# A transformer block's FFN in another order: the first row's gates ahead of the second row's products, the last row finished tile by tile, and the last sums on GpSimd

## The chip, the cores and the metric

The kernel runs on one core of one Trainium2 chip. Its engines work side by side, each through its own list of instructions: TensorE (PE, with its weight loads shown apart as PEld), VectorE (DVE), ScalarE (ACT) and GpSimd (POOL); SyncE (SP) issues most of the DMAs. The metric is the device time of one execution in microseconds (us); lower is better.

## What is computed

One transformer block on x of shape (2, 512, 512), all in float32: attention with 32 heads of 128, and then a feed-forward part that is a base product plus a gated mixture of eight low-rank experts. Each half is taken of the layer norm of x, and its own layer norm is added to x. Cut to what the change touches:

```python
def ffn(x, W_base, b_base, W_gate, W_thr, b_thr, A, B):
    base = x @ W_base.T + b_base
    adapted = softmax(x @ W_gate.T) - sigmoid(x @ W_thr.T + b_thr) / 8
    weights = maximum(adapted, 0)
    wsum = weights.sum(-1, keepdims=True)
    weights = weights / where(wsum == 0, 1, wsum)
    h = einsum('nd,erd->ner', x, A)          # 8 experts of rank 16
    return base + 2 * einsum('ner,ne,eor->no', h, weights, B)

x = x + layernorm(attention(layernorm(x)))
x = x + layernorm(ffn(layernorm(x)))
```

## The kernel before, in words

The two rows of the batch, b = 0 and 1, are each cut into NT = 4 tiles of 128 tokens by 512 features; NK = 4 is the number of 128-blocks of the feature dimension. The projections, the sums of the weights and the 64 rounds of attention (a round is one head of one row) come first and fill the first 1236 us. The change touches only what follows in `attention()` after the last round.

The block is built under a schedule in which PE, DVE, ACT and GpSimd run their instructions in the order in which the program writes them. So an instruction that waits holds back everything written after it on its engine, and "earlier in the text" means "earlier on the engine". Only SP's DMAs are placed by the scheduler.

PSUM, where PE leaves its products, is used as eight buffers of 128x512: four with the tag "ps" and four with the tag "aux" (`pt`). Each tag is a ring: the fifth tile of a tag takes the buffer of the first one, and its product waits until that one has been read.

The steps after the last round, for each row b:

- `outward` (L658): the last group's four products with Wo for each tile, psy; the sum `y` (L666) adds them to what earlier groups left.
- `residual` (called with "r"): `norms` over the four tiles of y, and then y = y * rs + (x + shift). This is the x of the second half, and stays in y.
- `norm_transposed`: `norms` again, ACT writes the normalized tile n_f, PE transposes its four blocks (nt_f), and four copies bring these out as nT_f, two by DVE (L164) and two by ACT (L166).
- the gate products hg (L798): one tile of 128 x 137 for each token tile: 128 hidden values h, 8 gate logits, 1 threshold. ACT copies them to hs (L801).
- the base products f (L806): four products for each token tile, left open in PSUM.
- the gates: a reduction for the maximum, two exponentials on ACT, some fourteen short DVE instructions, and then hw = h times its expert's weight for each token tile (L844).
- hT: PE transposes the four hw, ACT copies them out as hwT (L853).
- the expert products (L856): one more product on each of the four open f.
- z (L858): DVE adds the bias row; then `residual` with "z", whose result goes out by one DMA for each token tile (L862).

`norms` is a generator that all of these share. For each tile it issues bn_stats and bn_aggr on DVE and a square root on ACT (L144), and one tile later a reciprocal (L133) and the product `shift` = -mean * rs (L135) on DVE. `shift` is a scalar_tensor_tensor of 128x1: its two tensor inputs are the mean and rs.

Row 0's `ffn` uses "ps" for its transposes and its f, row 1's uses "aux" for its transposes; hg and hT use "aux" for both, and f uses "ps" for both. The second row's psy are in "aux", and their sums y are written behind the first row's copies nT_f. `ffn` is a generator in four parts, and the loop at the end of `attention()` interleaves the two rows with

```python
for part in (second, first, first, second, second):
    next(part)
```

that is: transposes of row 1, gates and hT of row 0, expert products of row 0, gate and base products of row 1, gates and hT of row 1, and then the rest of row 0 and of row 1. In it row 0's z statistics come on DVE behind row 1's gates, and row 1's four z come before any of its statistics.

ACT loads a table when its function changes between square root and exponential (ACT_TABLE_LOAD); copies and Identity need none. GpSimd has nothing to do after the last maximum of the attention (L528).

Of the kernel before, what the change touches and what calls it, by code (L numbers as in the profile page):

```python
# [9 lines left out]
F32 = mybir.dt.float32  # L10
AF = mybir.ActivationFunctionType
ALU = mybir.AluOpType
AX = mybir.AxisListType

P = 128
# [15 lines left out]
def kernel(ctx: ExitStack, tc: tile.TileContext, x, wq, wk, wv, wo, vecs, rows, wbase, gates, bexp, out):  # L31
# [33 lines left out]
    def tt(name):  # L65
        return tmp.tile([P, 512], F32, tag="tmp", name=name)

    def wide(name):
        return spool.tile([P, NT, 512], F32, tag="wide", name=name)
# [3 lines left out]
    def pt(name, tag=None):  # L73
        if tag is None:
            tag = ("ps", "aux")[turn_of[0] % 2]
            turn_of[0] += 1
        return psum.tile([P, 512], F32, tag=tag, name=name)
# [49 lines left out]
    def norms(srcs, name):  # L127

        waiting = []

        def ready():
            i, mv, rs = waiting.pop(0)
            nc.vector.reciprocal(rs, rs)  # L133
            shift = small.tile([P, 1], F32, tag="shift", name=f"shift_{name}_{i}")
            nc.vector.scalar_tensor_tensor(shift, mv[:, 0:1], -1.0, rs, ALU.mult, ALU.mult)  # L135
            return i, rs, shift

        for i, src in enumerate(srcs):
            st = small.tile([P, 6], F32, tag="st", name=f"st_{name}_{i}")
            mv = small.tile([P, 2], F32, tag="mv", name=f"mv_{name}_{i}")  # L140
            nc.vector.bn_stats(st, src)
            nc.vector.bn_aggr(mv, st)
            rs = small.tile([P, 1], F32, tag="rs", name=f"rs_{name}_{i}")
            nc.scalar.activation(rs, mv[:, 1:2], AF.Sqrt, bias=epst[:, 0:1], scale=1.0)  # L144
            waiting.append((i, mv, rs))
            if i > 0:
                yield ready()
        yield ready()

    def norm_transposed(tiles, name, tag):  # L150

        n = wide(f"n_{name}")
        pss = [pt(f"nt_{name}_{c}", tag) for c in range(NK)]
        for i, rs, shift in norms(tiles, name):
            nc.scalar.activation(n[:, i, :], tiles[i], AF.Identity, bias=shift, scale=rs)
            for c in range(NK):
                nc.tensor.transpose(pss[c][:, ts(i, P)], n[:, i, ts(c, P)], ident)

        def tiles_of():
            outs = []  # L160
            for c in range(NK):
                o = npool.tile([P, 512], F32, tag="nT", name=f"nT_{name}_{c}")
                if c % 2 == 0:
                    nc.vector.tensor_copy(o, pss[c])  # L164
                else:
                    nc.scalar.copy(o, pss[c])  # L166
                outs.append(o)
            return outs

        return tiles_of  # L170
# [134 lines left out]
    def attention():  # L305
# [351 lines left out]
        def y_tile(b, t):  # L657
            return y_pairs[b, t // 2][:, t % 2, :]  # L658

        def outward(g, b, t, tag=None):  # L660

            ps = pt(f"psy{b}_{g}_{t}", tag or "aux")
            for j in range(GH):
                o = os[b, g * GH + j]
                nc.tensor.matmul(ps, o[:, ts(t, P)], wos[g][j], start=(j == 0), stop=(j == GH - 1))  # L665
            return lambda: nc.vector.tensor_tensor(y_tile(b, t), ps, y_tile(b, t), ALU.add)  # L666
# [80 lines left out]
        )  # L747
        nc.sync.dma_start(out=gate_sb, in_=gates.rearrange("(c p) f -> p c f", p=P))
        nc.sync.dma_start(out=bexp_sb, in_=bexp)
        adds = [outward(NG - 1, 0, t, "ps") for t in range(NT)]  # L750
        for add in adds:
            add()
        adds = [outward(NG - 1, 1, t, "aux") for t in range(NT)]
        for b in range(B):
            x2 = [y_tile(b, t) for t in range(NT)]
            for _ in residual(again[b], x2, f"r{b}"):
                pass
            if b == 0:
                first = ffn(0, x2, wb, gate_sb, bexp_sb)
                next(first)  # L760
                for add in adds:
                    add()
                next(first)
            else:
                second = ffn(1, x2, wb, gate_sb, bexp_sb)

                for part in (second, first, first, second, second):
                    next(part)
                for _ in first:
                    pass  # L770
                for _ in second:
                    pass

    def residual(xts, ys, name):

        waiting = []

        def add():
            i, rs = waiting.pop(0)
            nc.vector.scalar_tensor_tensor(ys[i], ys[i], rs, xts[i], ALU.mult, ALU.add)  # L780
            return i

        for i, rs, shift in norms(ys, name):
            nc.scalar.activation(xts[i], xts[i], AF.Identity, bias=shift, scale=1.0)
            if waiting:
                yield add()
            waiting.append((i, rs))
        yield add()

    def ffn(b, xs, w, gate_sb, bexp_sb):  # L790

        xT = norm_transposed(xs, f"f{b}", "ps" if b == 0 else "aux")()
        yield
        hs = wide(f"hs{b}")[:, :, 0 : E * R + E + 1]
        for t in range(NT):
            ps = pt(f"hg{b}_{t}", "aux")
            for c in range(NK):
                nc.tensor.matmul(  # L798
                    ps[:, 0 : E * R + E + 1], xT[c][:, ts(t, P)], gate_sb[:, c, :], start=(c == 0), stop=(c == NK - 1)
                )  # L800
            nc.scalar.copy(hs[:, t, :], ps[:, 0 : E * R + E + 1])  # L801
        pss = []
        for t in range(NT):
            ps = pt(f"f{b}_{t}", "ps")
            for c in range(NK):
                nc.tensor.matmul(ps, xT[c][:, ts(t, P)], w[:, c, :], start=(c == 0), stop=False)  # L806
            pss.append(ps)
        yield

        def sm(name, n=NT):  # L810
            return small.tile([P, n], F32, tag=name, name=f"{name}{b}", bufs=1)

        def per_token(v):
            return v.unsqueeze(2).to_broadcast([P, NT, E])

        gl = hs[:, :, E * R : E * R + E]
        mx = sm("gmx")
        nc.vector.tensor_reduce(mx, gl, AX.X, ALU.max)
        ew = small.tile([P, NT, E], F32, tag="ew", name=f"ew{b}", bufs=1)
        nc.vector.tensor_tensor(ew, gl, per_token(mx), ALU.subtract)  # L820
        nc.scalar.activation(ew, ew, AF.Exp)
        thr = sm("thr")
        nc.scalar.activation(thr, hs[:, :, E * R + E], AF.Exp, bias=nbthr, scale=-1.0)
        nc.vector.tensor_scalar(thr, thr, 8.0, 8.0, ALU.mult, ALU.add)
        nc.vector.reciprocal(thr, thr)
        se = sm("gse")
        nc.vector.tensor_reduce(se, ew, AX.X, ALU.add)
        nc.vector.reciprocal(se, se)
        nc.vector.tensor_tensor(ew, ew, per_token(se), ALU.mult)
        nc.vector.tensor_tensor(ew, ew, per_token(thr), ALU.subtract)  # L830
        nc.vector.tensor_scalar(ew, ew, 0.0, None, ALU.max)
        ws = sm("gws")
        nc.vector.tensor_reduce(ws, ew, AX.X, ALU.add)
        iz = sm("giz")
        nc.vector.tensor_scalar(iz, ws, 0.0, None, ALU.is_equal)
        nc.vector.tensor_tensor(ws, ws, iz, ALU.add)
        nc.vector.reciprocal(ws, ws)
        nc.vector.tensor_scalar(ws, ws, 2.0, None, ALU.mult)
        nc.vector.tensor_tensor(ew, ew, per_token(ws), ALU.mult)

        pst = pt(f"hT{b}", "aux")
        for t in range(NT):
            hw = tt(f"hw{b}_{t}")
            nc.vector.tensor_tensor(  # L844
                hw[:, 0 : E * R].rearrange("p (e r) -> p e r", r=R),
                hs[:, t, 0 : E * R].rearrange("p (e r) -> p e r", r=R),
                ew[:, t, :].unsqueeze(2).to_broadcast([P, E, R]),
                ALU.mult,
            )
            nc.tensor.transpose(pst[:, ts(t, P)], hw[:, 0:P], ident)  # L850
        yield
        hT = tt(f"hwT{b}")
        nc.scalar.copy(hT, pst)  # L853
        zs = []
        for t in range(NT):
            nc.tensor.matmul(pss[t], hT[:, ts(t, P)], bexp_sb, start=False, stop=True)  # L856
            z = opool.tile([P, 512], F32, tag="o", name=f"z{b}_{t}")
            nc.vector.tensor_tensor(z, pss[t], bbase_b, ALU.add)  # L858
            zs.append(z)
        yield  # L860
        for t in residual(xs, zs, f"z{b}"):
            nc.sync.dma_start(out=out[b, ts(t, P), :], in_=zs[t])  # L862

    with tc.manual_schedule(engines=IN_ORDER):
        attention()
# [36 lines left out]
```

## Time and profile before

| | |
|---|---|
| three runs | 1334.28, 1334.54, 1338.74 us (median 1334.54) |
| the profiled execution | 1335.98 us |
| its span, first to last instruction | 1334.0 us |
| mean granted PE clock | 0.993 |
| busy: PE, DVE, ACT, POOL | 97%, 73%, 40%, 35% of the span |
| last round's weighted sum to the first transposes of row 0 | 1233 to 1264 us |
| from there to the end of the last product | 1264 to 1323 us |
| from there to the end of the span | 1323 to 1334 us |

The profile names an instruction by its line, engine and operation, and by the tiles that it writes and reads ("hT<-ident,hw" is the transposition of hw into hT). An f32 product appears as two records, so 16 products are "x32". A releaser (<-) is the instruction that ended a wait. Records of PE overlap a little and their ends are modelled; so the starts of the next ones are the safer measure.

The instructions of 128x512 elements that this part of the kernel is made of, from the page and the groups by form (mean, us): DVE sums 0.69, bn_stats 0.68, the DVE sum with a factor (scalar_tensor_tensor, L780) 0.75, ACT's normalization n_f 0.81, ACT copies 0.59, ACT's Identity with a shift 0.72, GpSimd's sums of the projections (L236) 1.30 and 1.38. A table load takes 1.28.

### The profile page before, as it was taken

To read this page: it belongs to the slowest core of one execution; us is meant where nothing else is said; L and a number is where in the kernel's file an instruction comes from. 1 tells how busy PE (TensorE), PEld (TensorE's weight loads), DVE (VectorE), ACT (ScalarE), POOL (GpSimd) and SP (SyncE) were. 2 spreads that over 40 slices of the span, in tenths; PEclk is the share of its full clock that TensorE was granted. 3 is DMA by queue.
4 is the path that set the end of the run, shared out by engine and by line. 5 is a ranking of instruction groups with operands and counts; after the bars stand their busy time and mean duration, and the time that the engine had idled before them with its cause. 6 is when DMAs were issued, how large, how long until landed. Compare 5 with 4: busy or idle time off the path is not lost.

```text
span 1334.0 us, 11818 instructions
## 1 busy us (share of the span) xinstructions
PE 1296.3 (97%) x3532; PEld 651.2 (49%) x3532; DVE 973.7 (73%) x1242; ACT 533.6 (40%) x736; POOL 472.1 (35%) x361
## 2 busy tenths in 40 slices
PE   7999999999999999999999999999999999999976
PEld 3444444444444444455555555555555555544443
DVE  7565654887565478888777787786787898899566
ACT  5222222322311234354454545545454655544333
POOL 4689897555762011111122222222222333211000
PEclk9999999999999999999999999999999999999988
DMA  7789978598997765533456565565656555511001
GB/s 286 245 317 309 342 269 274 198 328 298 334 324 258 249 201 182 180 122 101 153 150 172 152 185 153 144 189 163 161 154 186 146 134 134 127 64 38 26 1 63
DMA packets 146127, 250.45 MB, mean 188 GB/s; under 512 B 11792, under 2 KB 39568, under 8 KB 146064
## 3 DMA queue, kind: packets, MB, share of 16 engines
q1 hardware_dynamic: 135408, 230.31, 51.8%
q0 software_dynamic: 10080, 18.35, 8.4%
q10 hardware_dynamic: 576, 1.05, 0.2%
q8 instruction: 28, 0.46, 0.1%
q14 instruction: 35, 0.29, 0.1%
HBM read 147.43 MB, written 83.89 MB: 173 GB/s over the span
## 4 chain that ended last, share of the span: by engine, by line
PE 64%; DVE 6%; ACT 1%; issue 1%; ACTq 0%; DVEq 0%
PE pss L515 15%; PE o L571 15%; PE v L458 15%; PE psw L621 11%; PE psy L665 2%; PE f L806 2%; PE p_k L215 2%; DVE quarters L534 1%; DVE s L559 1%; ACT s L562 1%; PE f L856 1%; PE hg L798 1%; DVE y L655 1%; PE psd L548 1%; DVE m L525 1%
## 5 line engine op out<-in xcount | busy, mean ns | idle before, releaser
L528 POOL PARTITION_ALL_REDUCE top<-m x64 | 119.0, 1860 | 617.6 <-DVE m L526 617.6
L516 ACT ACTIVATE s<-pss,rk 128x512 f32<-128x512 f32 x256 | 175.9, 687 | 320.1 <-PE pss L515 314.6
L571 PE MATMUL o<-s,v 128*128 128x512 f32 x512 | 231.4, 594 | 5.9 <-ACT s L562 2.6
L515 PE MATMUL pss<-qh,kh 128*128 128x512 f32 x512 | 230.2, 592 | 0.0
L515 PEld LDWEIGHTS pss<-qh,kh 128*128 128x128 f32 x512 | 97.3, 190 | 122.4 <-issue 121.5
L571 PEld LDWEIGHTS o<-s,v 128*128 128x128 f32 x512 | 96.2, 190 | 112.0 <-issue 96.9
L534 DVE TRANSPOSE_TENSOR_REDUCE quarters<-s 128x64 f32<-128x2048 f32 x64 | 147.3, 2302 | 0.0
L559 DVE TENSOR_TENSOR s<-s,top 128x2048 f32<-128x2048 f32 x64 | 146.0, 2282 | 0.0
L562 ACT ACTIVATE s<-s 128x2048 f32<-128x2048 f32 x64 | 121.7, 1902 | 13.7 <-DVE s L559 13.6
L458 PE MATMUL v<-w_v,t 128*128 128x512 f32 x256 | 116.8, 600 | 0.0
L550 DVE RECIPROCAL inv<-psd 128x16 f32<-128x16 f32 x64 | 16.4, 256 | 127.5 <-PE psd L548 127.5
L235 ACT ACTIVATE sq_k<-k 128x512 f32<-128x512 f32 x62 | 38.6, 630 | 137.6 <-DVE k L288 65.8
L236 POOL TENSOR_TENSOR accq<-accq,sq_q 128x512 f32<-128x512 f32 x62 | 80.7, 1303 | 35.5 <-ACT sq_q L235 33.7
L236 POOL TENSOR_TENSOR acck<-acck,sq_k 128x512 f32<-128x512 f32 x62 | 85.4, 1381 | 22.1 <-ACT sq_k L235 19.0
L235 ACT ACTIVATE sq_q<-q 128x512 f32<-128x512 f32 x62 | 38.9, 631 | 134.0 <-DVE q L288 69.2
L458 PE MATMUL v<-w_v,nT_a 128*128 128x512 f32 x192 | 88.3, 601 | 0.0
L621 PE MATMUL psw<-wr,oh 128*128 128x256 f32 x384 | 88.3, 380 | 0.0
L215 PE MATMUL p_k<-t,s_k 128*128 128x512 f32 x192 | 85.0, 592 | 0.0
L215 PE MATMUL p_q<-t,s_q 128*128 128x512 f32 x192 | 85.0, 592 | 0.0
L621 PEld LDWEIGHTS psw<-wr,oh 128*128 128x128 f32 x384 | 72.5, 190 | 19.8 <-issue 11.5
L525 DVE TENSOR_TENSOR m<-s 128x1024 f32<-128x1024 f32 x64 | 77.8, 1216 | 4.7 <-ACT s L516 4.7
L458 PEld LDWEIGHTS v<-w_v,t 128*128 128x128 f32 x256 | 46.7, 190 | 49.3 <-issue 49.0
(180 smaller groups left out, 1774.5 us busy)
## 6 DMA issues: line engine op xcount, KB each, us to landing
keptq<-q SPq DMA_DIRECT2D x64, 256.0 KB, 6.5
q<-keptq SPq DMA_DIRECT2D x16, 1024.0 KB, 6.5
w_v<-keptw SPq DMA_DIRECT2D x32, 512.0 KB, 4.0
keptk<-k SPq DMA_DIRECT2D x64, 256.0 KB, 6.4
keptqs<-q SPq DMA_DIRECT2D x64, 256.0 KB, 6.6
qh<-keptqs SPq DMA_DIRECT2D x64, 256.0 KB, 3.0
kh<-keptk SPq DMA_DIRECT2D x64, 256.0 KB, 2.7
keptv<-o_v SPq DMA_DIRECT2D x64, 256.0 KB, 3.7
```

The source lines that it names most:

```text
L215: nc.tensor.matmul(ps, a[:, c, ts(j, P)], x[c], start=(c == 0), stop=(c == 1))
L236: nc.gpsimd.tensor_tensor(accs[b], accs[b], sq, ALU.add)
L458: nc.tensor.matmul(ps, x[c][:, ts(t, P)], w[:, c, :], start=(c == 0), stop=(c == 1))
L515: nc.tensor.matmul(ps, kk[i][:, ts(k, P)], qs[i], start=True, stop=True)
L516: nc.scalar.activation(s[:, k, :], ps, AF.Copy, scale=rks[b][:, k : k + 1])
L525: nc.vector.tensor_tensor(m, s[:, 0:2, :], s[:, 2:4, :], ALU.max)
L528: nc.gpsimd.partition_all_reduce(ms[i], m[:, 0, :], P, ReduceOp.max)
L534: nc.vector.tensor_reduce(quarters.rearrange("p k j -> p (k j)"), ss[i].rearrange("p k (j r) -> p (k j) r", r=32), AX.X, ALU.add, apply_tr ...
L559: nc.vector.tensor_tensor(s, s, top.unsqueeze(1).to_broadcast([P, NT, 512]), ALU.subtract)
L562: nc.scalar.activation(ss[i], ss[i], AF.Exp)
L571: nc.tensor.matmul(po, vs[b, c][:, k, ts(j, P)], ss[i][:, k, :], start=(k == 0), stop=(k == NT - 1))
L621: nc.tensor.matmul(ps[:, t, :], a, right_of[i, g][:, j, :], start=(j == 0), stop=(j == 1))
```

## The change

`ffn` becomes a class with one method for each step, and the caller writes out the order. The order at the end of `attention()`:

```diff
-        adds = [outward(NG - 1, 0, t, "ps") for t in range(NT)]
-        for add in adds:
+        x2s = [[y_tile(b, t) for t in range(NT)] for b in range(B)]
+        first, second = (Ffn(b, x2s[b], wb, gate_sb, bexp_sb) for b in range(B))
+        adds = [[outward(NG - 1, b, t, ("ps", "aux")[b]) for t in range(NT)] for b in range(B)]
+        for add in adds[0]:
             add()
-        adds = [outward(NG - 1, 1, t, "aux") for t in range(NT)]
-        for b in range(B):
...
-                for part in (second, first, first, second, second):
-                    next(part)
-                for _ in first:
-                    pass
-                for _ in second:
-                    pass
+        residual(again[0], x2s[0], "r0")
+        first.norm()
+        first.turn()
+        first.gate_products()
+        for add in adds[1]:
+            add()
+        residual(again[1], x2s[1], "r1")
+        first.base(range(NT))
+        second.norm()
+        first.gates()
+        second.turn()
+        first.hidden()
+        second.gate_products()
+        first.experts(range(NT))
+        first_z = list(first.z())
+        second.gates()
+        second.base(range(2))
+        second.hidden()
+        second.base(range(2, 3))
+        second.experts(range(3))
+        second.base(range(3, NT))
+        second.experts(range(3, NT))
+        first.finish(first_z)
+        second.finish(second.z(), direct=(NT - 1,))
```

Transposes, gate products and hT of both rows now use "ps", and the base products of both rows use "aux". Two token tiles share one PSUM tile of gate products, and so one ACT copy:

```diff
+            for u in range(NT // 2):
+                ps = pt(f"hg{b}_{u}", "ps")[:, 0 : 2 * W].rearrange("p (t f) -> p t f", t=2)
...
+                nc.scalar.copy(self.hs[:, ts(u, 2), :], ps)
```

The gates are the same instructions as before, in `gates()`, with the four hw at their end; `hidden()` is the transposes and the copy hwT, now in a tile of `opool`. The finish is new. `z()` is a generator, so that for row 1 each tile's z comes directly before that tile's bn_stats; for row 0 the four z are made at once, as `first_z`. Of the eight last sums seven go to GpSimd, on a z that ACT has normalized in place; the last tile of row 1 keeps the way it had:

```diff
+            for t, rs, shift in norms(coming(), f"z{self.b}"):
+                z, x2 = got[t], self.xs[t]
+                if t in direct:
+                    nc.scalar.activation(x2, x2, AF.Identity, bias=shift, scale=1.0)
+                    nc.vector.scalar_tensor_tensor(z, z, rs, x2, ALU.mult, ALU.add)
+                else:
+                    nc.scalar.activation(z, z, AF.Identity, bias=shift, scale=rs)
+                    nc.gpsimd.tensor_tensor(z, z, x2, ALU.add)
+                nc.sync.dma_start(out=out[self.b, ts(t, P), :], in_=z)
```

As built, GpSimd's list gets, behind the last maximum of the attention, one more unnamed instruction and the seven sums; the lists of the other engines hold the same work in the new order, four copies hs less on ACT, and the stores keep their order on SP.

More of the change, by code (lines that the diff above doesn't have):

```diff
@@ L749, in attention @@
         nc.sync.dma_start(out=bexp_sb, in_=bexp)
-        adds = [outward(NG - 1, 0, t, "ps") for t in range(NT)]
-        for add in adds:
+        x2s = [[y_tile(b, t) for t in range(NT)] for b in range(B)]
+        first, second = (Ffn(b, x2s[b], wb, gate_sb, bexp_sb) for b in range(B))
+        adds = [[outward(NG - 1, b, t, ("ps", "aux")[b]) for t in range(NT)] for b in range(B)]
+        for add in adds[0]:
             add()
-        adds = [outward(NG - 1, 1, t, "aux") for t in range(NT)]
-        for b in range(B):
-            x2 = [y_tile(b, t) for t in range(NT)]
-            for _ in residual(again[b], x2, f"r{b}"):
-                pass
[L758 to L765, printed above, removed]
-                for part in (second, first, first, second, second):
-                    next(part)
-                for _ in first:
-                    pass
-                for _ in second:
-                    pass
+        residual(again[0], x2s[0], "r0")
[22 more added lines that the diff above has]
+        second.finish(second.z(), direct=(NT - 1,))
     def residual(xts, ys, name):
@@ L780, in add @@
             nc.vector.scalar_tensor_tensor(ys[i], ys[i], rs, xts[i], ALU.mult, ALU.add)
-            return i
         for i, rs, shift in norms(ys, name):
@@ L785, in residual @@
             if waiting:
-                yield add()
+                add()
             waiting.append((i, rs))
[L788 to L799, printed above, removed]
-                )
[L801 to L862, printed above, removed]
@@ new lines, in residual, with __init__, norm, turn @@
+        add()
+    class Ffn:
+        def __init__(self, b, xs, w, gate_sb, bexp_sb):
+            self.b, self.xs, self.w, self.gate_sb, self.bexp_sb = b, xs, w, gate_sb, bexp_sb
+            self.pss = {}
+        def norm(self):
+            self.turned = norm_transposed(self.xs, f"f{self.b}", "ps")
+        def turn(self):
+            self.xT = self.turned()
+        def gate_products(self):
+            b, W = self.b, E * R + E + 1
+            self.hs = wide(f"hs{b}")[:, :, 0:W]
+            for u in range(NT // 2):
+                ps = pt(f"hg{b}_{u}", "ps")[:, 0 : 2 * W].rearrange("p (t f) -> p t f", t=2)
+                for t in range(2):
+                    for c in range(NK):
+                        x = self.xT[c][:, ts(2 * u + t, P)]
+                        nc.tensor.matmul(ps[:, t, :], x, self.gate_sb[:, c, :], start=(c == 0), stop=(c == NK - 1))
+                nc.scalar.copy(self.hs[:, ts(u, 2), :], ps)
+        def base(self, tiles):
+            for t in tiles:
+                ps = self.pss[t] = pt(f"f{self.b}_{t}", "aux")
+                for c in range(NK):
+                    nc.tensor.matmul(ps, self.xT[c][:, ts(t, P)], self.w[:, c, :], start=(c == 0), stop=False)
+        def gates(self):
+            b, hs = self.b, self.hs
+            def sm(name, n=NT):
+                return small.tile([P, n], F32, tag=name, name=f"{name}{b}", bufs=1)
+            def per_token(v):
+                return v.unsqueeze(2).to_broadcast([P, NT, E])
+            gl = hs[:, :, E * R : E * R + E]
+            mx = sm("gmx")
+            nc.vector.tensor_reduce(mx, gl, AX.X, ALU.max)
+            ew = small.tile([P, NT, E], F32, tag="ew", name=f"ew{b}", bufs=1)
+            nc.vector.tensor_tensor(ew, gl, per_token(mx), ALU.subtract)
+            nc.scalar.activation(ew, ew, AF.Exp)
+            thr = sm("thr")
+            nc.scalar.activation(thr, hs[:, :, E * R + E], AF.Exp, bias=nbthr, scale=-1.0)
+            nc.vector.tensor_scalar(thr, thr, 8.0, 8.0, ALU.mult, ALU.add)
+            nc.vector.reciprocal(thr, thr)
+            se = sm("gse")
+            nc.vector.tensor_reduce(se, ew, AX.X, ALU.add)
+            nc.vector.reciprocal(se, se)
+            nc.vector.tensor_tensor(ew, ew, per_token(se), ALU.mult)
+            nc.vector.tensor_tensor(ew, ew, per_token(thr), ALU.subtract)
+            nc.vector.tensor_scalar(ew, ew, 0.0, None, ALU.max)
+            ws = sm("gws")
+            nc.vector.tensor_reduce(ws, ew, AX.X, ALU.add)
+            iz = sm("giz")
+            nc.vector.tensor_scalar(iz, ws, 0.0, None, ALU.is_equal)
+            nc.vector.tensor_tensor(ws, ws, iz, ALU.add)
+            nc.vector.reciprocal(ws, ws)
+            nc.vector.tensor_scalar(ws, ws, 2.0, None, ALU.mult)
+            nc.vector.tensor_tensor(ew, ew, per_token(ws), ALU.mult)
+            self.hws = []
+            for t in range(NT):
+                hw = tt(f"hw{b}_{t}")
+                nc.vector.tensor_tensor(
+                    hw[:, 0 : E * R].rearrange("p (e r) -> p e r", r=R),
+                    hs[:, t, 0 : E * R].rearrange("p (e r) -> p e r", r=R),
+                    ew[:, t, :].unsqueeze(2).to_broadcast([P, E, R]),
+                    ALU.mult,
+                )
+                self.hws.append(hw)
+        def hidden(self):
+            pst = pt(f"hT{self.b}", "ps")
+            for t in range(NT):
+                nc.tensor.transpose(pst[:, ts(t, P)], self.hws[t][:, 0:P], ident)
+            self.hT = opool.tile([P, 512], F32, tag="o", name=f"hwT{self.b}")
+            nc.scalar.copy(self.hT, pst)
+        def experts(self, tiles):
+            for t in tiles:
+                nc.tensor.matmul(self.pss[t], self.hT[:, ts(t, P)], self.bexp_sb, start=False, stop=True)
+        def z(self):
+            for t in range(NT):
+                z = opool.tile([P, 512], F32, tag="o", name=f"z{self.b}_{t}")
+                nc.vector.tensor_tensor(z, self.pss[t], bbase_b, ALU.add)
+                yield z
+        def finish(self, zs, direct=()):
+            got = []
+            def coming():
+                for z in zs:
+                    got.append(z)
+                    yield z
+            for t, rs, shift in norms(coming(), f"z{self.b}"):
[7 more added lines that the diff above has]
+                nc.sync.dma_start(out=out[self.b, ts(t, P), :], in_=z)
```

## The prediction

> **What bounds the kernel now.** I read the page first: TensorE (PE) is busy for 97% of the span, but its digits fall in the last two of 40 slices, and PEclk is 8 there. The change touches nothing before that, so I went on to the chain of waits between 1285 and 1334 us (start us, length us, what):
>
> ```profile
> 1285.66 1.54 PE nt_f L157 x14
> ...
> 1292.69 0.30 DVE hw L844
> ...
> 1293.13 1.10 PE hT L850 x4
> ...
> 1294.95 5.54 PE f L856 x8
> 1300.49 3.76 PE hg L798 x32
> 1304.25 13.73 PE f L806 x32
> ...
> 1319.15 3.71 PE f L856 x8
> ...
> 1329.93 0.75 DVE z L780
> ```
>
> The chain leaves PE twice. After the transposes nt_f it runs through the copies and the first row's gate arithmetic, during which PE has nothing to do. After the last expert product (1322.86) it runs through DVE and ACT, 7.8 us with PE finished. The waits of that stretch (us in total, times, longest) give the first gap, and a smaller one before the gate products:
>
> ```profile
> PE hT L850 <- DVE hw L844: 5.7, 1, 5.7
> PE hg L798 <- DVE y L666: 1.6, 1, 1.6
> ```
>
> The gap has a second price. The eight f L856 records take 5.54 us the first time and 3.71 the second, and the four hT 1.10 against 0.45. The windows of one or two us say why (after the bounds: length, PE, PEld, DVE, ACT, POOL busy with counts, then granted clock, DMA share, GB/s):
>
> ```profile
> 1289.00:1291.00 2.00, 0.00 (x0) 0.00 (x0) 0.80 (x6) 1.02 (x3) 0.00 (x0) 1.00 0.00 0
> 1291.00:1293.00 2.00, 0.00 (x0) 0.00 (x0) 1.73 (x10) 0.00 (x0) 0.00 (x0) 0.72 0.00 0
> 1293.00:1294.00 1.00, 0.87 (x4) 0.69 (x4) 0.59 (x3) 0.00 (x0) 0.00 (x0) 0.50 0.00 0
> 1298.00:1299.00 1.00, 1.00 (x2) 0.28 (x2) 0.23 (x1) 0.00 (x0) 0.00 (x0) 0.65 0.00 0
> ```
>
> The clock stays 1.00 until 1291, nearly 4 us into the idleness, then drops to 0.50 and comes back between 1298 and 1299. So the gap costs its length and about 2.4 us of slow products (0.65 on hT, 1.8 on f).
>
> **The change, step by step** (times on the scale of the profiled execution).
>
> *Gate products of row 0.* Today they wait for the second row's y, because they use the "aux" buffers; in the change they use "ps" and wait only for the copies nT_f. The DVE copy of the third ends at 1267.25. From there 14 of 16 products are left, at 0.24 us each (32 records in 3.86 us): end at 1270.65 instead of 1271.76. Gain 1.1. The base products now need y's buffers, freed from 1267.85 on, so that wait costs nothing. The two wider copies of 274 elements have no row; between 0.28 (137 elements) and 0.59 (512) I take 0.4. They end near 1271.2, so the second row's residual chain, whose first square root ran at 1272.13 behind the four narrow copies, moves up by 1.0.
>
> *Gates of row 0 "early".* The base products run 1270.65 to 1284.4 and the transposes of row 1 to 1286.3. On DVE the gates come behind the second row's norm, which ends at 1281.5 (today 1282.5). Their exponentials stand on ACT behind n_f's last tile (1283.6 - 1.0 = 1282.6) and a table load of 1.28, and end at 1284.3. From there to hw is 2.6 us and four hw are 0.9 (1290.06, 1292.69, 1293.6 today): hw done at 1287.9. So the gates are not wholly hidden. Queued behind them on DVE are the copies nT_f of row 1, ready since 1286.0, which now run at 1287.8 and 1288.4. The hT transposes take the "ps" buffer that the first copy frees: they start at 1288.5. PE's gap is 2.2 us instead of 5.7. The clock held for nearly 4 us above, so I charge no slow products.
>
> *PE from there.* hT 0.6; gate products of row 1 from 1289.1 (second copy) to 1293.0, which hide the copy hwT (0.73 wait today); eight expert records at 0.43, to 1296.4. Today the base products of row 1 start at 1304.25. **Gain so far 7.85**: 1.1 + 3.5 + 2.4 + 0.7, and 0.15 of rounding. The rest of PE's work is unchanged: base tiles 0 and 1 to 1303.3 (16 x 0.43), hT 0.45 (its hw are ready from 1301.0: after the z at 1297.3 come 4.35 us of gates, as 1304.59 to 1308.94 today), tile 2 to 1307.2, experts of tiles 0 to 2 to 1309.7, tile 3 and its expert to 1314.0. The copy hwT hides behind tile 2. Against 1322.86 that is 8.8 earlier.
>
> *The finish, alone.* Row 0's statistics stand on ACT behind hwT (1303.96 to 1304.55) and a table load: first square root at 1305.85. DVE has done two bn_stats by then and waits. From there a tile costs DVE 1.07: bn_stats 0.72, aggregate 0.10, reciprocal 0.16, shift 0.09. Row 1's tile adds z, 0.71, in all 1.78, and its last tile alone runs on DVE to the end. The bound from below: if GpSimd (POOL) did not touch DVE, row 0 would end at 1308.9, z of tile 3 would meet its product at 1314.33, and the last sum would end at 1318.5.
>
> *The sums on POOL.* Seven adds of 128x512, row of the trace L236: 1.27 us median, against 0.74 for the DVE sum they replace. [...] The trace says the price is elsewhere. Where POOL adds while DVE normalizes, at 13 to 20 us (start us, length us):
>
> ```profile
> 13.55 0.68 DVE L141 BATCH_NORM_STATS2 st_a<-x 128x6 f32<-128x512 f32 x1
> 13.58 1.27 POOL L189 TENSOR_TENSOR s_q<-s_q,w_q 128x512 f32<-128x512 f32 x1
> 14.81 1.26 POOL L190 TENSOR_TENSOR s_q<-w_q 128x512 f32<-128x512 f32 x1
> 15.32 0.77 DVE L135 SCALAR_TENSOR_TENSOR shift_a<-mv_a,rs_a 128x1 f32<-128x1 f32 x1
> 18.61 1.26 POOL L189 TENSOR_TENSOR s_q<-s_q,w_q 128x512 f32<-128x512 f32 x1
> 18.75 1.13 DVE L135 SCALAR_TENSOR_TENSOR shift_a<-mv_a,rs_a 128x1 f32<-128x1 f32 x1
> ```
>
> bn_stats keeps its 0.68 beside an add. The shift, 0.16 us elsewhere, ends with the add: 15.32 + 0.77 = 16.09 and 14.81 + 1.26 = 16.07; 19.88 and 19.87. Reciprocals and aggregates are not held. [...] So I put the adds in: the first is ready at 1307.5 (shift at 1306.3, ACT's normalization 0.81 as n_f, 0.14 to POOL as between ACT and POOL at 41.4), the next three each 1.23 apart. Shifts 2 and 3 of row 0 wait 0.3 and 1.0: z of row 1 starts at 1310.05, 1.75 after its product (1308.3). Its adds start at 1314.4, 1316.8 and 1319.2; shifts 1 and 2 wait 0.63 each; shift 3 at 1318.3; ACT's pass over x2 behind that of tile 2, to 1319.8; the last sum waits for the last add, 1320.5, and takes 0.74: **1321.3**. The first shift races the first add by under 0.1 us; lost, the end is 1322.2.
>
> *GpSimd's switch.* The built order has one unnamed GpSimd instruction ahead of the first add, as it has one before the first add and the first partition_all_reduce today. No row times it. From below it is 0; from above, the idle time in which today's ran: 11.4 us before the first add, 35.5 before the first all_reduce. It is issued once the last all_reduce ends (1227.7), 80 us before the first add. I take 0, from this cover.
>
> *DMA.* The eight stores stay on SP in the same order, row 0's four now near 1309 to 1312.5, away from the last. The tail from last sum to end is 3.3 us (1330.68 to 1334.0), as today.
>
> **Sum.** 1330.7 - 1321.3 = 9.4 us off the span, on PE's side 7.85 and the rest in the finish. The profiled execution took 1335.98; the median shown is 1334.54, 1.4 lower. I subtract from the median: **1325.2 us**, -0.7%.
>
> **The rivals.** A difference under about 0.5% (6.7 us) can't be told from none here.
> 1. *POOL and DVE hardly meet.* The end is 1318.5, gain 12.2: 1322.3. For it: most DVE work of the finish has one SBUF input. Against it: all four shifts beside adds at 15 to 20 us were held. 15%.
> 2. *PE's gap stays long.* The gates of row 0 come later than I put them, by a hand-over or two, and the clock drops before hT: another 2.4 us of slow products, or as much delay. For it: the gap is 2.2 us even on paper, and everything behind it moves one for one. 1327.6. 13%.
> 3. *The finish becomes serial on POOL.* Every two-input instruction waits its add out: at most 7 x 1.26 = 8.8 us over 1318.5, end 1327.3, gain 3.4: 1331.1. The gain won on PE is given back. For it: wo sums beside adds at 115 us took 1.64 instead of 0.69. Against: shifts are one in five of the instructions. 8%.
> 4. *The switch of GpSimd comes late*: slower. If it were done only at the first add, 1307.5, each us beyond what the finish can hide comes on top; POOL's seven adds would have to follow it. At 20 us, inside the bounds, POOL ends at 1307.5 + 20 + 8.8 = 1336.3, and the last sum at 1337.1, 6.4 us later than today: 1341. It decides against the change from about 14 us. For it: no row shows the switch. Against: it has no wait and 80 us. 4%.
>
> **How the numbers follow.** Forecast 60%, its own spread 1323.5 to 1328. The range 1321.5 to 1329 leaves out cases 3 and 4. Faster by over 0.5% (below 1327.9): nearly all of the forecast, case 1, half of case 2: 0.77. Slower: case 4, 0.04. Same: 0.19.
>
> **What would show it.** Right: hT of row 0 starts near 1288.5 and its expert products take 3.7, at clock 1.00; hwT of row 1 near 1304; some shifts of row 1 last 0.6 to 1.3 us and end with a POOL add; last sum about 1.5 long. Wrong: a PE gap over 4 us, shifts of 0.16 throughout, or a first POOL add long after its ACT pass.

## The result, and the profile after

| | before | after |
|---|---|---|
| median of seven runs each, side by side | 1337.69 us (1333.53 to 1340.32) | 1324.55 us (1322.21 to 1330.41) |
| the profiled execution shown | 1335.98 us | 1322.88 us |
| its span | 1334.0 us | 1321.1 us |
| mean granted PE clock | 0.993 | 0.997 |
| first product psy of the last group starts at | 1236.79 us | 1232.32 us |
| from there to the end of the last sum on DVE: **the last stretch** | 93.89 us | 84.91 us |

The ratio of the times is 0.9913, with a 95% interval of 0.9888 to 0.9938: the change saves 8.3 to 15 us. The forecast was 9.4.

The fifth row of the table is a warning. Of the 12.9 us between the two spans, 4.5 lie ahead of the first instruction that the change touches. (The stretch itself gives 9.0, and what follows its last sum is 0.6 longer after the change: 3.9 us in place of 3.3.) The 4.5 us were there as early as the first maximum of the attention. First before, then after, from the timeline of GpSimd (start us, length us, engine, line, operation, tiles, and in brackets the idle time before it with what ended it):

```profile
447.35 1.80 POOL L528 PARTITION_ALL_REDUCE top<-m  x1 [35.49 <-DVE m L526]
```

```profile
442.87 1.81 POOL L528 PARTITION_ALL_REDUCE top<-m  x1 [34.67 <-DVE m L526]
```

Other executions put it at 448.58 (the program of before) and at 446.89 and 448.74 (that of after), and the start of the last stretch lies between 1232.3 and 1240.6 in the ten experiments and these two, whatever the kernel. So the 4.5 us are drift of the projections from execution to execution, and not the change. From here on I compare the last stretch alone. The two profiles differ by 9.0 us in it.

Most of that is on PE. The chain of waits of the kernel after (start us, length us, what):

```profile
1282.59 0.90 DVE hw L862 x4
1283.49 0.61 DVE nT_f L164
1284.14 5.81 PE hg L816 x32
1289.95 3.43 PE f L879 x8
1293.38 6.87 PE f L823 x16
...
1301.33 1.28 ACT L144
...
1305.75 1.02 DVE shift_z L135
...
1315.99 1.24 DVE z L900
```

and the wait that was 5.7 us before:

```profile
PE hT L873 <- DVE hw L862: 1.2, 1, 1.2
```

The gates of row 0 still stand in the chain (hw, and one copy nT_f behind it), but PE now idles 1.2 us ahead of hT and not 5.7, and the eight expert records of row 0 take 3.43 us in place of 5.54: the slow products are gone from there. One row is not as forecast: the second row's gate products take 5.81 us where before took 3.76. The windows of one us tell why (length, PE, PEld, DVE, ACT, POOL busy, then granted clock, DMA share, GB/s):

```profile
1282.00:1283.00 1.00, 0.00 (x0) 0.01 (x1) 0.90 (x6) 0.76 (x2) 0.00 (x0) 1.00 0.03 8
...
1285.00:1286.00 1.00, 1.00 (x7) 1.00 (x7) 0.00 (x0) 0.00 (x0) 0.00 (x0) 0.57 0.00 0
...
1287.00:1288.00 1.00, 1.00 (x7) 1.00 (x6) 0.00 (x0) 0.39 (x1) 0.00 (x0) 0.50 0.00 0
1288.00:1289.00 1.00, 1.00 (x8) 1.00 (x8) 0.00 (x0) 0.00 (x0) 0.00 (x0) 0.72 0.00 0
```

PE is busy without a break from 1285, and the clock is nevertheless at half speed from 1285.1 to 1288.6.

The rest is the finish. The timeline of the kernel after, DVE's shifts and last sum, one of its z, and GpSimd's adds:

```profile
1304.25 4.96 POOL L903 TENSOR_TENSOR z<-z,y 128x512 f32<-128x512 f32 x4 [81.03 <-ACT z L902]
1305.28 0.26 DVE L135 SCALAR_TENSOR_TENSOR shift_z<-mv_z,rs_z 128x1 f32<-128x1 f32 x1
1305.75 1.02 DVE L135 SCALAR_TENSOR_TENSOR shift_z<-mv_z,rs_z 128x1 f32<-128x1 f32 x1
1306.69 0.68 DVE L884 TENSOR_TENSOR z<-f,row 128x512 f32<-128x512 f32 x1
...
1311.01 1.26 POOL L903 TENSOR_TENSOR z<-z,y 128x512 f32<-128x512 f32 x1 [1.80 <-PE f L879]
1311.71 0.58 DVE L135 SCALAR_TENSOR_TENSOR shift_z<-mv_z,rs_z 128x1 f32<-128x1 f32 x1
...
1314.61 0.16 DVE L135 SCALAR_TENSOR_TENSOR shift_z<-mv_z,rs_z 128x1 f32<-128x1 f32 x1
1315.42 1.26 POOL L903 TENSOR_TENSOR z<-z,y 128x512 f32<-128x512 f32 x1 [0.94 <-ACT z L902]
1315.99 1.24 DVE L900 SCALAR_TENSOR_TENSOR z<-z,rs_z,y 128x512 f32<-128x512 f32 x1 [1.23 <-ACT y L899]
```

Take the row at 1311.71: it is a product of 128x1, and it ends at 1312.29, just as the add that began at 1311.01 ends (1312.27). At 1314.61, with GpSimd idle, the same instruction takes 0.16. The last sum took 0.75 on DVE before and takes 1.24 beside an add. The z at 1306.69 lies wholly beside the row of four adds and keeps its 0.68; its two inputs are f, in PSUM, and the bias row, in SBUF. And the first add starts 0.09 us after ACT's pass over its z (1303.35 to 1304.16), so no wait of GpSimd's own is seen there.

The end of the program pays for the adds once. The last sum on DVE ends 3.9 us before the end of the span; before it was 3.3, and so it is in every kernel below without sums on GpSimd (3.3), while every one with them has 3.9. In the records of the trace, GpSimd's DRAIN, with which it closes, ends at 1320.32, 3.64 us after its last add, and SyncE, whose own DRAIN ends at 1319.88, goes on only behind it, at 1320.49. In the kernels without these sums GpSimd's first DRAIN is over by 1236.

### The profile page after: what moved, and what is told of

Same layout as the page of the kernel before. It is cut to its first block, busy times and chain, and to the rows that moved or that the text cites. A ratio compares the mean times of both kernels' runs of the same rounds, so it can differ in the third digit from the quotient of the medians.

```text
span 1321.1 us, 11827 instructions
## 1 busy us (share of the span) xinstructions
PE 1294.2 (98%) x3532; PEld 651.5 (49%) x3532; DVE 973.5 (74%) x1235; ACT 533.4 (40%) x732; POOL 481.7 (36%) x368
## 4 chain that ended last, share of the span: by engine, by line
PE 90%; DVE 7%; ACT 2%; DMA 1%; issue 1%; SPq 0%; ACTq 0%; DVEq 0%
PE pss L515 15%; PE o L571 15%; PE v L458 15%; PE p_q L215 15%; PE p_k L215 15%; PE psw L621 10%; PE psy L665 2%; DVE quarters L534 1%; DVE s L559 1%; PE hg L816 1%; ACT s L562 1%; DVE y L655 1%; PE psd L548 1%; PE f L823 1%; DVE m L525 1%
## 5 line engine op out<-in xcount | busy, mean ns | idle before, releaser
L562 ACT ACTIVATE s<-s 128x2048 f32<-128x2048 f32 x64 | 121.7, 1902 | 13.7 <-DVE s L559 13.6
L235 ACT ACTIVATE sq_q<-q 128x512 f32<-128x512 f32 x62 | 38.9, 630 | 132.8 <-DVE q L288 69.1
```

The costliest lines, as they stand in the source:

```text
L562: nc.scalar.activation(ss[i], ss[i], AF.Exp)
```

## The experiments

Three theories were to be told apart. The forecast's: about 8 us come from PE's earlier start on the second row's base products, and about 1.5 from the finish, in which two-input instructions of DVE wait out GpSimd's adds. The first rival: the move to GpSimd is what pays (or costs), and the order pays little. The second: the whole difference is one of execution to execution. All figures below are of the last stretch unless they are called totals; what its longer end costs (0.6 wherever GpSimd has last sums) is not in them.

### Both programs again

No edit: the kernel before, and the kernel after.

> The kernel before, unchanged. I call the stretch from the first of the 64 psy records to the end of the last sum the last stretch: 93.9 us in the first profile of the kernel before, 84.9 in that of the change; it began at 1236.8 and at 1232.3. Theory (the 4.5 us ahead of it are a difference between executions, made in the projections): the last stretch is 93.9 within 0.3 again, and its start lies anywhere between 1231 and 1238. Rival (the change also speeds up what lies ahead): start at 1236 to 1237.5 here, and 1232 to 1233 in every kernel with the new order.

> The changed kernel, unchanged. Theory on the clock [...]: the gate products of row 1 take 5.8 us again or 3.9 where the clock stays 1.00, and the last stretch 84.9 or 83. Rival (chance): a different duration each time. Start of the last stretch as in the first run: 1231 to 1238 by the theory of drift, 1232 to 1233 by its rival.

Measured: before 94.04 us (93.89 the first time), after 83.25 (84.91 the first time). Totals 1337.15 and 1325.26. The difference is not chance: the stretch of before repeats within 0.2 us while its totals move by more: 1329.81 and 1337.15 for the same program on the same chip.

The second execution of after is 1.66 shorter than the first. From the timeline of PE:

```profile
1287.05 0.84 PE L873 MATMUL hT<-ident,hw 128*128 128x128 f32 x4 [1.16 <-DVE hw L862]
1288.17 4.15 PE L816 MATMUL hg<-gate_sb,nT_f 128*128 128x137 f32 x32 [0.27 <-DVE nT_f L164]
1292.16 3.60 PE L879 MATMUL f<-bexp_sb,hwT 128*128 128x512 f32 x8
```

The gaps ahead of hT and hg, 1.16 and 0.27, are the same in both executions. The gate products take 4.15 here and took 5.81 there, and 5.81 - 4.15 = 1.66 is the whole difference. So the clock fell in one and not in the other, after the same gaps.

### The shift with one tensor input

```diff
-            nc.vector.scalar_tensor_tensor(shift, mv[:, 0:1], -1.0, rs, ALU.mult, ALU.mult)
+            nc.vector.tensor_scalar(shift, mv[:, 0:1], rs, -1.0, ALU.mult, ALU.mult)
```

> The change, with shift written as a tensor_scalar: mean times the scalar rs times -1, one tensor input in place of two. Theory (a VectorE instruction with two tensor inputs waits out the GpSimd sum that runs): every shift of the finish takes 0.16 to 0.2, the last sum, which keeps two inputs, still waits; the finish is shorter by the 0.1 + 0.86 of row 0 and 0.83 of row 1, less what z of the last tile then waits for PE: last stretch about 1.5 shorter, 83.4. Rival (any VectorE instruction that reads a second operand, a pointer too, waits): shifts of 0.3 to 1.0 remain, last stretch 84.9.

Measured: 82.24 us, 1.0 less than the kernel after at the same clock (83.25), where 1.5 was expected. The timeline, of the same instructions as above:

```profile
1303.23 4.96 POOL L903 TENSOR_TENSOR z<-z,y 128x512 f32<-128x512 f32 x4 [79.80 <-ACT z L902]
1304.31 0.21 DVE L135 TENSOR_SCALAR shift_z<-mv_z,rs_z 128x1 f32<-128x1 f32 x1
1304.79 0.21 DVE L135 TENSOR_SCALAR shift_z<-mv_z,rs_z 128x1 f32<-128x1 f32 x1
...
1309.29 1.26 POOL L903 TENSOR_TENSOR z<-z,y 128x512 f32<-128x512 f32 x1 [1.09 <-ACT z L902]
1309.99 0.21 DVE L135 TENSOR_SCALAR shift_z<-mv_z,rs_z 128x1 f32<-128x1 f32 x1
...
1313.54 1.24 DVE L900 SCALAR_TENSOR_TENSOR z<-z,rs_z,y 128x512 f32<-128x512 f32 x1 [0.95 <-ACT y L899]
```

No shift waits any more: rs is given as a scalar operand and not as a tensor, and each takes 0.21 us beside a running add. The last sum still has two tensor inputs, and still takes 1.24. So what held the shift is the second tensor input, and not the add beside it as such. The z above, not held (0.68) with one of its two tensors in PSUM, narrows it: the instructions that were held have both in SBUF. The kind of operation does not decide it: z is a tensor_tensor and keeps its 0.68, and the wo sums that the prediction quotes, tensor_tensor with both inputs in SBUF, took 1.64 beside adds. From row 1's hT to the end the stretch is 1.38 us shorter (15.76 against 17.14). It gives 0.37 of that back: the form takes 0.21 where the old one takes 0.16 when nobody disturbs it, it stands in every norm, and the first row's gates, which are on the path, come later by about that much (row 0's hT 51.08 us after the start of the stretch, against 50.70).

### All sums on DVE

First with the means that the change has itself:

```diff
-        first.finish(first_z)
+        first.finish(first_z, direct=range(NT))
...
-        second.finish(second.z(), direct=(NT - 1,))
+        second.finish(second.z(), direct=range(NT))
```

> The change, with all eight last sums on VectorE as scalar_tensor_tensor (ACT's pass goes to x2 in each tile), nothing on GpSimd. Theory (VectorE is the bound of the finish, and GpSimd takes more off it than its waits give back): no shift over 0.2; row 0 costs VectorE 4 x 0.66 more and 0.96 of waits less, row 1 3 x 0.66 more and 0.83 less, the last sum 0.5 less: last stretch 2.3 longer, 87.2. Rival (the waits eat the gain): 84.9 or less.

Measured: 91.22 us, a miss by 4. The waits say what was built:

```profile
DVE z L900 <- ACT y L899: 6.3, 8, 0.8
```

Each of the eight sums stood directly behind ACT's pass over the same tile, and held up the statistics of the next tile for 0.8 us. This measures that wait and not GpSimd. The second form writes each sum one tile later, so that ACT's pass lies beside the statistics of the next tile:

```diff
             for t, rs, shift in norms(coming(), f"z{self.b}"):
...
-                    nc.scalar.activation(z, z, AF.Identity, bias=shift, scale=rs)
-                    nc.gpsimd.tensor_tensor(z, z, x2, ALU.add)
...
+                nc.scalar.activation(x2, x2, AF.Identity, bias=shift, scale=1.0)
+                if waiting:
+                    add()
+                waiting.append((t, rs))
+            add()
```

where `add()` is DVE's sum with a factor, and the store, of the oldest tile in `waiting`.

> The change, tile by tile, but all sums on VectorE, each one tile late, so that none waits for its ACT pass (in the run with the sums on VectorE at once, each waited 0.79 for ACT, which hid the question). Theory: VectorE is the bound; row 0 leaves it at 74.3, a tile of row 1 costs it 2.44 in place of 1.78, less 0.83 of waits: last stretch 84.9, 1.7 over the change at clock 1.00 (83.25). Rival (the waits of shift for GpSimd give the gain back): 83.3 or less.

Measured: 86.23 us, with gate products of 5.81. It has to be set against the execution of after with the same slow products, 84.91: GpSimd is worth **1.3 us** of the stretch, where 1.7 was expected. The longer end of the program takes 0.6 of that back, so to the end of the span it is 0.7 (one execution of each). So GpSimd pays a little, and it is not the main cause of the 9 us.

### One half of the change at a time

The new order with the finish of before (all four z of row 1 ahead of its statistics, sums on DVE):

```diff
-        def finish(self, zs, direct=()):
...
+        def finish(self, zs):
+            for t in residual(self.xs, zs, f"z{self.b}"):
+                nc.sync.dma_start(out=out[self.b, ts(t, P), :], in_=zs[t])
```

> The change up to the expert products, with the finish as before: all four z of row 1 first, then the statistics, all sums on VectorE one tile late, as residual does. Read beside the second run of the change, whose clock stayed 1.00 (last stretch 83.25). Theory (most of the gain is PE's, the finish gives the smaller part): VectorE leaves row 0 5.45 after its first square root, at 74.3 after the start of the stretch; the last z waits for PE until 77.1; from there 7.8 as before: last stretch 84.9, so the new finish is worth 1.7. Rival (the tile by tile finish and GpSimd are the main gain): 88 or more.

Measured: 86.49 us, with gate products of 5.81, so the order alone saves 93.9 - 86.5 = 7.4 of the 9.0 us that the two first profiles differ by, and the finish the 1.6 that are left (86.49 - 84.91). Of these 1.6, the z tile by tile give 0.3 without GpSimd (86.49 - 86.23), and GpSimd's sums the 1.3 above.

The new finish with the gates of row 0 where they were, behind the second row's transposes, and the second row's gate products behind the first row's experts:

```diff
         first.base(range(NT))
         second.norm()
-        first.gates()
         second.turn()
+        first.gates()
         first.hidden()
-        second.gate_products()
         first.experts(range(NT))
+        second.gate_products()
```

> The change, with the gates of row 0 behind the copies nT_f of row 1 and its gate products behind the expert products of row 0, the order of the kernel before; the finish as in the change. Theory: PE's gap before hT is 5 us again, the clock falls to 0.50 in it, hT takes 1.1 and the expert products 5.5, the copy hwT is bare: 4.9 longer, last stretch 88.1 (83.25 + 4.9). Rival (the gap is covered elsewhere once the finish is new): 85 or less.

Measured: 91.09 us, 7.8 more than after at full clock, where less was expected. The timeline of PE:

```profile
1293.93 1.08 PE L873 MATMUL hT<-ident,hw 128*128 128x128 f32 x4 [5.72 <-DVE hw L862]
1295.69 6.47 PE L879 MATMUL f<-bexp_sb,hwT 128*128 128x512 f32 x8 [0.68 <-ACT hwT L875]
```

The gap is that of before again, 5.72 us; then come 0.68 for hwT, which no product hides, and expert records of 6.47 us in place of 3.60. Against the kernel after at full clock that is 4.56 + 0.68 + 2.87 = 8.1; gate products without the wait of 0.27 ahead of them bring it to the 7.8. The expectation had left out a part of the gap and of the slow products. The two halves need not add up: in this kernel the clock was at 0.50 for 10.2 us, in before for 6.8, so the 2.8 by which it beats before is not a clean measure of the finish.

### The gap filled

With the gap of 1.16 us left over, the question is whether the rest of it, and the fall of the clock, can be had too. The last base tile of row 0 is held back until row 1's norm, the gates are cut in two (`logits()` up to the exponentials), and the second row's first gate products stand ahead of hT. The second row's square-root table is loaded ahead of its gates, and the shift has one tensor input:

```diff
-        first.base(range(NT))
+        first.base(range(NT - 1))
         second.norm()
-        first.gates()
+        first.base(range(NT - 1, NT))
+        first.logits()
         second.turn()
+        first.gates()
+        second.gate_products(range(1))
         first.hidden()
-        second.gate_products()
+        second.gate_products(range(1, NT // 2))
         first.experts(range(NT))
         first_z = list(first.z())
-        second.gates()
+        second.logits()
+        nc.scalar.activation(root, epst[:, 0:1], AF.Sqrt)
+        second.gates()
```

> The change with four edits: the fourth base tile of row 0 behind the transposes of row 1, which fills PE's gap; the copies nT_f of row 1 in the time in which VectorE waits for the exponentials; hT between the two halves of row 1's gate products; shift with one tensor input; and a square root on a constant behind the exponentials of row 1, so that the table load comes early. Theory: PE reaches the base products of row 1 1.65 earlier than in the second run of the change at any phase of the clock, the table load leaves row 0's finish, shifts take 0.2: last stretch 80.6. Rival (the finish is bound by VectorE and gains nothing from an earlier PE): 82.2, as with one-input shifts alone.

Measured: 80.33 us. The timeline of PE and, below it, one window of 22 us over it all:

```profile
1283.56 3.60 PE L829 MATMUL f<-wb,nT_f 128*128 128x512 f32 x8
1286.99 2.04 PE L822 MATMUL hg<-gate_sb,nT_f 128*128 128x137 f32 x16
1288.87 0.60 PE L888 MATMUL hT<-ident,hw 128*128 128x128 f32 x4
1289.31 2.05 PE L822 MATMUL hg<-gate_sb,nT_f 128*128 128x137 f32 x16
1291.19 3.60 PE L894 MATMUL f<-bexp_sb,hwT 128*128 128x512 f32 x8
```

```profile
1278.00:1300.00 22.00, 21.61 (x89) 12.69 (x88) 14.63 (x60) 10.26 (x20) 0.00 (x0) 1.00 0.00 1
```

None of these rows has an idle time in brackets. In the whole window PE is busy for 21.61 of 22 us (0.34 of the rest is a wait of the transposes nt_f for ACT, ahead of these rows), and the clock is 1.00 throughout. Against the kernel after, the stretch is 2.9 us shorter at full clock and 4.6 where the clock fell. Of the 2.9, the shift with one tensor input gives 1.0 (82.24, above); the other edits, which were not tried apart, give 1.9, and 1.8 of these are there when PE reaches the base products of row 1 (57.85 us after the start of the stretch, against 59.61 with that shift alone).

To see what of this the total shows, it and the kernel after were timed in five rounds beside before:

> The kernel with the gap filled, again, timed. Last stretch 80.3 again, at clock 1.00 throughout; against the kernel before (93.9 to 94.0) 13.6 us less, a ratio of 0.9898, with an interval of some 0.003 each way, since what lies ahead of the last stretch differs by up to 8 us from one execution to another.

> The changed kernel, timed on the same chip beside it. Last stretch 83.3 or 84.9, by the clock; ratio to the kernel before between 0.9920 and 0.9932 (9.0 to 10.7 us of 1337), if the projections' drift cancels; 2 to 4 us over the kernel with the gap filled, about what the interval is.

| | total, median | ratio to before (1332.53) | last stretch |
|---|---|---|---|
| the gap filled | 1321.51 us (1318.57 to 1324.22) | 0.9920 (0.9905 to 0.9934) | 80.33 us |
| the kernel after | 1321.95 us (1318.87 to 1327.09) | 0.9928 (0.9910 to 0.9947) | 83.24 us |

Both stretches repeat to 0.01 us those seen at full clock. In the totals the 2.9 us do not stand out from the drift ahead of the stretch: most of each interval lies in the other. The gap's filling is shown in the stretch, and not in the total. The ratio expected for it, 0.9898, lies outside the interval that was measured: of the 13.6 us of the stretch, 0.6 go to the longer end of the program, and why the totals show only some 11 is not known.

## Why the prediction was right, and where it was not

The forecast of 9.4 us lies inside the measured 8.3 to 15, and the last stretch gives 9.0 for the first execution of after and 10.7 for the other two (93.9 or 94.0, less 83.2). Less the 0.6 of the longer end that is 8.4 and 10.1. The mechanism was right too: most of the gain comes from PE's shorter gap, and in the finish two-input instructions of DVE wait out GpSimd's adds. The steps, in us from the start of the stretch (1236.79 on the forecast's scale, 1232.32 in the first execution of after):

| step of the prediction | forecast | measured, first execution | at full clock |
|---|---|---|---|
| gate products of row 0 done, base products start | 33.9 | 33.9 | |
| exponentials of row 0 end | 47.5 | 47.6 | |
| four hw done | 51.1 | 51.2 | |
| hT of row 0 starts | 51.7 | 50.7 | 50.7 |
| base products of row 1 start (by the chain) | 59.6 | 61.1 | 59.4 |
| first square root of the finish | 69.1 | 70.3 | 68.6 |
| end of the last sum | 84.5 | 84.9 | 83.3 |

- *Gate products of row 0*, 1.1 us, and *Gates of row 0 early* up to hw: within 0.2. The forecast's decision that the gates are **not** wholly hidden, since row 1's norm and ACT's table load (1.28) stand ahead of them, was right.
- *hT behind the first copy of DVE*: wrong by 1.0. The step let hT wait for the buffer that the first DVE copy nT_f frees. In after hT starts at 1283.03, and that copy at 1283.40; hT waits for hw; its buffer had been freed by ACT's copies (1281.68 to 1282.75), for which its weight load waits by the profile. The gap is 1.2 and not 2.2. From hT to the gate products it then took 1.1 us and not 0.6, with 0.27 of it for the second copy.
- *No slow products charged*: wrong in the first execution, right in others. The clock fell for 3.41 us and cost 1.66. The step took the time for which the clock had held (in fact until 1291.87 in before, 4.5 us after the last transposition) as what any gap may last. In after the clock fell with only 1.16 and 0.27 us of idleness ahead of it; why it fell was not shown. This is rival 2's second price in another place: rival 2 looked for it on the expert products, after a gap over 4 us. With the 1.0 won on hT, 0.5 lost behind it and this lost, PE's gain was 6.4 us (67.46 - 61.06) in the first execution and 8.1 at full clock; the forecast's 7.85 lies between.
- *The sums on POOL*: right in kind and in size. The four waits were put at 0.3, 1.0, 0.63 and 0.63; measured (the row less 0.16) they are 0.10, 0.86, 0.42 and 0.41. Row 1's first z was to start 4.2 us after the first square root, and started 4.07 after it. The one-input shift shows the cause. A sum is longer on GpSimd (1.26 against 0.74), but where DVE bounds the finish, the move gained 1.3 in the stretch, and 0.7 to the end of the span.
- *The last sum waits for the last add, then takes 0.74*: off in form. It started 0.57 us into the add, and took 1.24 in all, ending 0.55 after the add's end. So this two-input sum of 128x512 is slowed by 0.5, where the forecast had it wait 0.7.
- *GpSimd's switch*, put at 0: no wait for one is seen. In the records of the trace two MODIFY_POOL_CONFIG of 0.09 us each (1223.17 and 1223.20) stand ahead of GpSimd's first sum, 81 us before it; what they do was not shown. Rival 4 falls. *The tail*, 3.3: it was 3.9 (1317.23 to 1321.1), since the end of the program waits for GpSimd's DRAIN; the prediction had put GpSimd's closing at nothing.
- *Rival 1* (no meeting of DVE and POOL) falls by the four waits, *rival 3* (all serial) by the one-input instructions, which kept their lengths.

Errors of opposite signs helped the figure. By the table, in the first execution: hT 1.0 early, from hT to the gate products 0.5 late, the clock 1.7 late, and from the first square root to the last sum 14.6 us in place of 15.4; together they leave 0.4. That part was luck. That the forecast's total also met the measured median (1325.2 and 1324.55) owes something to drift: the second set of runs put both kernels elsewhere (1332.53 and 1321.95).

## What to carry to other kernels

Compare the stretch that the change touches, from a product ahead of it to its end: here that repeats to 0.2 us as long as the clock agrees, while the totals of one program differ by up to 8. Here a second engine took over sums from the one that bounds the stretch, and though each is longer on it, 1.26 us in place of 0.74, the stretch was 1.3 shorter. Look at what is left beside it: with a scalar operand in place of a second tensor in SBUF the short products no longer waited, and that gave another 1.0. Count what the second engine adds at the end of the program: here 0.6 of 1.3 us went there. A gap on TensorE is best filled with products that are ready, since its length was not its only price: in before 5.7 us of it came with some 2.4 us more for the products behind it, while the clock stood at 0.50.

## What the runs showed of the hardware

**The clock fell after a short gap, and not each time.** The order of the change has gaps of 1.16 us (1.53 with the one-input shift) and 0.27 us ahead of and among 5 us of narrow work. Behind them the clock fell to 0.50 in three profiled executions (after, the old finish, the later sums on DVE), 2.11, 2.22 and 1.85 us after row 0's hT had started, and the gate products took 5.81 us. In four (after again, the one-input shift, the sums on DVE at once, after timed) they took 4.15 or 4.16; in the first of these the clock was 1.00 from 1270 to 1300 us. The short falls last 3.41 us each, and those after the long gaps 6.83 twice (before) and 10.2 (late gates): one, two and three times 3.41. In before and after the clock falls once more behind the last product, at 1326.00 and 1315.86 us, 34.13 and 30.72 after the fall just named: ten and nine times 3.413.

What decides between the executions was not shown: the gaps ahead of hT are the same within 0.01 us in six of the seven, and no run set anything else. In the first execution with the gap filled the clock was 1.00 from 1278 to 1300 us, in the second from 1270 to 1300; two executions don't show that it always holds. The source of the drift in the projections stays open too.

**Which DVE instructions a GpSimd add holds.** In these runs those with at most one tensor in SBUF kept their lengths beside it: bn_stats (0.68 to 0.70), aggregates (0.18), reciprocals (0.13 to 0.16), a product of a tensor with a scalar operand (0.21), and z, whose other tensor is in PSUM (0.68). With two tensors in SBUF, a product of 128x1 that started 0.7 us into an add lasted to the add's end (0.58 in place of 0.16), and a sum of 128x512 grew from 0.75 to 1.24.
